# A graph-attention kernel: a planner that keeps VectorE's two-operand steps and GpSimd's sums apart, five places for streamed factors in the last group, and beta x W2 off TensorE

## The chip, the cores and the metric

The kernel runs on one core of a Trainium2 chip, all in float32. The metric is device time in microseconds (us), the median of three runs.

## What is computed

128 graphs of 64 nodes with 512 features each pass through four layers. Each layer adds to x what it makes of h = relu(layernorm(x)). Cut to what matters:

```python
# layer 0: two hypergraph convolutions with a layer norm between, H = (adj != 0)
h1 = relu(Dn * H @ (Be * H.T @ (h @ W1.T)) + b1)
h1 = layer_norm(h1) * gamma + beta
x += Dn * H @ (Be * H.T @ (h1 @ W2.T)) + b2 + h
# layer 1: s = h @ w @ a; A = exp(lrelu(8*tanh((s_i + s_j)/8))) * adj, its rows made to sum to those of adj
x += A @ h @ w
# layer 2: attention
P = adj * exp(q @ k.T)              # q = h @ Wq.T + bq, k = h @ Wk.T + bk
x += (P / P.sum(-1)) @ (h @ Wv.T + bv)
# layer 3: t = normalized adj * exp(lrelu(si + sj + ab)), from h @ Wv3
x += relu(sum over k = 0, 1, 2 of (t^k @ h) @ Wk3[k] + bk3[k])
```

Dn and Be are the reciprocal degrees of nodes and hyperedges. The term beta @ W2.T is a constant row. The kernel makes it once, at the start.

## The kernel before

**Tiling.** A group is 8 graphs: four tiles x of 128 rows (two graphs) by 512. There are 16 groups. All groups pass through layers 0 and 1 first (stage one) and are stored to DRAM (xm, L885). Then all pass through layers 2 and 3 (stage two), where x is read back (x_mid, L346 and L986). The large products are written as Strassen products. L682 is the matmul of layers 0 and 1, whose operand sums are VectorE's (L674). L921 is that of layer 2, with its sums at L907, and L1112 that of layer 3. L583 multiplies a tile by a block-diagonal 128x128 matrix of edge weights, which VectorE writes (L864 in layer 1).

**Layer 3's factors.** The seven combinations of Wk3 are made in stage one and stored to DRAM (fac). In stage two each group streams all of them in again, in 14 loads at L1104: seven of 768 KB (four blocks) and seven of 576 KB (three). They go into places named wf, of which there are three. A place is free again when the matmuls at L1112 that read it are done. Each load needs the place and, by the planner's rule, nothing else. Ahead of these products a group makes its transition matrix t (scores L750 to L756, exponential L1012, L1013 to L1019, 32x32 transposes L1027), its square (L1037, copied at L1039), and t h and t^2 h (L1058). Scores go from a column to a row by way of DRAM (across: a store at L720, two loads at L724); for the last group TensorE does that (L742).

**Who sums.** VectorE makes Strassen sums in SBUF with two SBUF operands (L674, L907, L1082, L1095 to L1097), also L382 (dot products), L700, L864, L960 and L1147. Its other steps read one operand from PSUM (L652, L654, L702, L712, L877, L1131, L996). GpSimd, which is POOL in the profile, has wide sums in SBUF (L710, L798, L799, L876, L973, L1126, L1140 to L1143) and three small steps on single columns for each layer norm (L555, L556, L561).

**The order.** No loop order of the program decides when something runs. Every step is put into a graph (Graph.op) with its engine, a cost in us, what it reads and writes, and a priority. Graph.run plays the steps through in a model of the engines: at every turn it takes the step that can start first, of equals the one of least priority number, and gives it a buffer. The model's start times then set the order in which all instructions are issued, each engine working in order. A step's result counts as there after its cost and a latency (for DMAs, cost is the time on SP's queue). The priority numbers come from a table AT with one entry for each part of the program, from STRETCH (how fast the number grows within a layer) and from PERIOD1 and PERIOD2 (how far groups are apart). The model knows one resource per engine; it lets a VectorE step and a GpSimd step run at the same time whatever they read.

Where the model leaves TensorE idle for over 1 us with a free PSUM bank, fill issues dummy matmuls on a matrix of ones (L1187), FILL = 0.75 of the gap.

**The start.** setup_l0 makes beta x W2 with 8 matmuls of one output row each (L438, two instructions each), copies the row (L440), scales W2 by gamma in place on ScalarE (L442), and spreads the row over 128 partitions with a matmul of ones (L443, copied at L444). bq_c, the first load of all, is a 2 KB load. setup_l3 and setup_bq make small vectors from weights that are loaded in tmp tiles.

Of the kernel before, what the change touches and what calls it, by code (L numbers as in the profile page):

```python
# [11 lines left out]
ALU = mybir.AluOpType  # L12
AX = mybir.AxisListType

P = 128
# [20 lines left out]
class Op:  # L36
    __slots__ = ("eng", "cost", "fn", "prio", "bufs", "npre", "succ", "ready", "seq", "lat")


class Graph:  # L40
# [11 lines left out]
    def op(self, eng, cost, fn, r=(), w=(), lat=None):  # L52
        o = Op()
        o.lat = self.LATENCY[eng] if lat is None else lat
# [28 lines left out]
    def run(self, slots, after, fill):  # L83
# [17 lines left out]
        at = dict.fromkeys(self.ENGINES, 0.0)  # L101
# [4 lines left out]
        while left:  # L106
            best = None
            for e in self.ENGINES:

                can = []  # L110
                for o in open_[e]:
                    t = max(o.ready, at[e])
# [26 lines left out]
            at[o.eng] = t + o.cost  # L139
            end = t + o.cost + o.lat  # L140
# [28 lines left out]
def tile_adj_preln_d4(  # L169
# [95 lines left out]

    def act(cost, fn, r, w):
        return G.op("ACT", cost, fn, r, w)

# [6 lines left out]
    def quad(b):  # L275
        return b.t.rearrange("p (c k) -> p c k", c=4)

    FILL, LAT = 0.75, 2.5


    STRETCH, PERIOD1, PERIOD2 = (1.9884, 2.1221, 50.9861, 3.7462), 79.959, 161.557
    AT = {
        "x0": -2165.99, "apart": 359.07, "w1": 560.57, "b1": -128.79, "w2": 2266.0, "w": 629.08, "c1": 83.74, "l0":
        -235.81, "c2": 158.31, "l1": 2264.36, "c": -2424.06, "g0": -2117.86, "g1": -2122.8, "g2": -1819.53, "g3":
        -591.79, "g": -1886.72, "bq": -99.87, "l3": -7.89, "wg": -1139.97, "wp": 573.47, "beg0": -142.55, "beg1":
        62.01, "end00": -13.21, "end01": -32.01, "end11": -18.15, "new2": -7.11, "new3": -54.85, "end2": -9.77,
        "end3": 676.8, "load1": 485.14, "load2": 547.59, "m": -43.8, "h0": -30.46, "p0": -0.2, "z0": -80.08, "q0":
        9.15, "y0": -548.45, "h1": -32.41, "p1": -27.07, "z1": -26.16, "q1": -1.17, "y1": 3.58, "s": -28.4, "t0":
        14.62, "e0": 9.6, "t1": 5.71, "e1": -125.7, "hT": 311.43, "sh": 220.57, "lq": 604.06, "pt": 684.45, "v":
        70.12, "pv": 723.21, "s3": 659.55, "tt": 692.85, "a0": 741.32, "b0": -508.03, "a1": 777.21, "ws": 323.28,  # L290
        "load3": 129.62, "bk": 350.9,
    }

    def part(name):
        G.shift = AT[name]
# [42 lines left out]
    def load_group(g, src, apart=0.0):  # L338
        b = Buf("adj")
        dma(256, lambda: nc.sync.dma_start(b.t, adj[g]), [], [b])  # L340
        adjs[g] = b
        for t in range(T):
            xx = Buf("x")
            at, key = src(g, t)
            G.shift += apart
            dma(256, lambda xx=xx, at=at: nc.sync.dma_start(xx.t, at), key, [xx], lat=LAT if src is x_mid else 2.0)  # L346
            xt[g, t] = xx
# [7 lines left out]

    part("x0")
    bq_c = load_cols("bq_c", bq, KD)
# [22 lines left out]
    def dot(in0, in1, acc, r, w):  # L380
        j = Buf("o")
        dve(0.77, lambda: nc.vector.scalar_tensor_tensor(j.t, in0(), 1.0, in1(), op0=ALU.mult, op1=ALU.mult,  # L382
                                                         accum_out=acc()), r, [*w, j])

    def combine(name, w_, x_, kc, n, eng, olds=()):
# [5 lines left out]
        cost = c_v(kc * n) * (1 if eng == "DVE" else 2)  # L391
        low, high = wkeys(name, 0, kc), wkeys(name, kc, 2 * kc)
        T1 = (name, "T1")
        G.op(eng, cost, lambda: sub(x_[:, 1], blk(1, 1), blk(0, 1)), [*low, *high], [(name, "x1"), *olds])
        G.op(eng, cost, lambda: sub(blk(0, 1), blk(0, 1), blk(0, 0)), [*low, (name, "x1")], [T1, (name, "given")])
        G.op(eng, cost, lambda: sub(x_[:, 0], blk(1, 1), blk(0, 1)), [*high, T1], [(name, "x0")])
        G.op(eng, cost, lambda: sub(x_[:, 2], blk(1, 0), x_[:, 0]), [*high, (name, "x0")], [(name, "x2")])
# [6 lines left out]
    def combine_hT(name, w_, x_, left):  # L404
# [9 lines left out]
        v = lambda fn, r, w: dve(c_v(D), fn, r, w)  # L414
# [17 lines left out]
    def setup_l0():  # L432

        p, row, pb = Buf("ps"), Buf("o"), Buf("ps")

        def mm():
            for c in range(KH):
# [873 lines left out]
```

## Time and profile before

| what | value |
|---|---|
| median of three runs | 2346.6 us (2346.2 to 2349.21) |
| the profiled execution: its time, its span | 2347.34 us, 2345.6 us |
| TensorE clock granted, mean | 0.998 of full |
| busy: TensorE, VectorE, ScalarE, GpSimd | 2301.3, 1936.0, 1386.6, 1201.9 us |
| filler matmuls (L1187) | 226, 29.3 us busy |
| DMA: moved in all, busy share in 1300-2200 us | 355 MB, 0.81 |
| factor loads, issue to landing | 768 KB 5.8 us, 576 KB 5.0 us (medians) |

Busy time is the union of an engine's instructions. Matmuls are pipelined and their ends are modelled, so the prediction takes the spacing of their starts. Stage one fills the span to about 1200 us and stage two the rest, with groups overlapping at the seam. A group line reads: line, engine, operation, output and inputs by tile name, shapes, count, busy time, mean ns of one, idle time just before and what ended it. A tile name with underscores is memory that several tiles share in turn: w2m_wm_a_wf holds the weights of stage one first, and then a3 and the factor places.

### The profile page before, as it was taken

To read this page: it belongs to the slowest core of one execution; us is meant where nothing else is said; L and a number is where in the kernel's file an instruction comes from. 1 tells how busy PE (TensorE), PEld (TensorE's weight loads), DVE (VectorE), ACT (ScalarE), POOL (GpSimd) and SP (SyncE) were. 2 spreads that over 40 slices of the span, in tenths; PEclk is the share of its full clock that TensorE was granted. 3 is DMA by queue.
4 is the path that set the end of the run, shared out by engine and by line. 5 is a ranking of instruction groups with operands and counts; after the bars stand their busy time and mean duration, and the time that the engine had idled before them with its cause. 6 is when DMAs were issued, how large, how long until landed. Compare 5 with 4: busy or idle time off the path is not lost.

```text
span 2345.6 us, 39929 instructions
## 1 busy us (share of the span) xinstructions
PE 2301.3 (98%) x14342; PEld 1876.8 (80%) x14342; DVE 1936.0 (83%) x4004; ACT 1386.6 (59%) x1986; POOL 1201.9 (51%) x1764
## 2 busy tenths in 40 slices
PE   9999999999999999999999999999999999999998
PEld 4676667776777767777688989999999999999998
DVE  7977887878878777787867888888889888888886
ACT  4656565665656756557556656655565656556642
POOL 5435566556565455553433554455455545455533
PEclk9999999999999999999999999999999999999999
DMA  7333342432333432223334888787888888798767
GB/s 265 85 76 74 82 103 72 106 83 72 95 84 99 89 77 69 70 73 66 89 89 134 235 230 224 211 223 207 242 231 220 230 213 215 211 252 227 214 184 234
DMA packets 403478, 355.13 MB, mean 151 GB/s; under 512 B 290896, under 2 KB 321872, under 8 KB 403280
## 3 DMA queue, kind: packets, MB, share of 16 engines
q1 hardware_dynamic: 403280, 352.58, 56.2%
q8 instruction: 113, 1.85, 0.3%
q14 instruction: 85, 0.70, 0.1%
HBM read 241.05 MB, written 44.33 MB: 122 GB/s over the span
## 4 chain that ended last, share of the span: by engine, by line
PE 75%; DMA 9%; DVE 9%; ACT 3%; POOL 2%; issue 2%; SPq 0%; DVEq 0%; POOLq 0%; ACTq 0%
PE ps L682 35%; PE ps L921 13%; PE ps L1112 13%; PE ps L583 5%; DMA w2m_wm_a_wf<-fac 4%; PE ps L1058 2%; PE ps L990 2%; DVE o L382 2%; PE ps L835 2%; DMA x<-xm 2%; PE ps L952 1%; DVE st L553 1%; DMA wa_q<-o 1%; PE ps L468 1%; DMA rw<-row 1%
## 5 line engine op out<-in xcount | busy, mean ns | idle before, releaser
L574 ACT ACTIVATE h<-x,nm,rs 128x512 f32<-128x512 f32 x384 | 307.0, 814 | 260.7 <-POOL nm L561 234.8
L1112 PE MATMUL ps<-w2m_wm_a_wf 128*128 128x128 f32 x2304 | 300.0, 276 | 3.8 <-DMA w2m_wm_a_wf<-fac 3.1
L1112 PEld LDWEIGHTS ps<-w2m_wm_a_wf 128*128 128x128 f32 x2304 | 279.4, 192 | 9.0 <-issue 2.0
L555 POOL TENSOR_SCALAR rs<-mv 128x1 f32<-128x1 f32 x320 | 102.5, 320 | 349.0 <-DVE mv L554 329.6
L682 PE MATMUL ps<-w2m_wm_a_wf,s_s_zz 128*128 128x256 f32 x1152 | 279.8, 380 | 0.7 <-DVE s_s_zz L674 0.5
L1112 PE MATMUL ps<-w2m_wm_a_wf,tmp_mB_xi 128*128 128x128 f32 x2016 | 262.3, 275 | 3.3 <-ACT h L574 1.7
L682 PEld LDWEIGHTS ps<-w2m_wm_a_wf,s_s_zz 128*128 128x128 f32 x1152 | 216.4, 190 | 48.1 <-issue 18.7
L1112 PEld LDWEIGHTS ps<-w2m_wm_a_wf,tmp_mB_xi 128*128 128x128 f32 x2016 | 244.9, 192 | 6.1 <-ACT h L574 3.0
L682 PE MATMUL ps<-w2m_wm_a_wf,rT_vu_tt 128*128 128x256 f32 x1024 | 237.2, 379 | 3.7 <-ACT rT_vu_tt L594 3.6
L682 PE MATMUL ps<-wa_mem,mT_sx 128*128 128x512 f32 x512 | 236.6, 593 | 0.2 <-ACT mT_sx L585 0.2
L682 PEld LDWEIGHTS ps<-w2m_wm_a_wf,rT_vu_tt 128*128 128x128 f32 x1024 | 193.2, 190 | 44.6 <-issue 12.4
L556 POOL TENSOR_TENSOR rs<-rs,mhalf 128x1 f32<-128x1 f32 x320 | 213.5, 667 | 26.6
L553 DVE BATCH_NORM_STATS2 st<-x 128x6 f32<-128x512 f32 x256 | 173.2, 680 | 17.0 <-DMA x<-xm 11.2
L682 PE MATMUL ps<-wa_mem,s_s_zz 128*128 128x512 f32 x384 | 180.0, 597 | 0.5 <-DVE z_hT L702 0.4
L682 PEld LDWEIGHTS ps<-wa_mem,mT_sx 128*128 128x128 f32 x512 | 96.9, 190 | 102.0 <-issue 96.6
L561 POOL TENSOR_SCALAR nm<-mv,rs 128x1 f32<-128x1 f32 x320 | 160.9, 504 | 30.4
L710 POOL TENSOR_TENSOR u<-u,row_sh 128x256 f32<-128x256 f32 x96 | 77.7, 822 | 170.7 <-DVE u L652 142.3
L592 ACT COPY o<-h 128x1024 uint16<-128x1024 uint16 x128 | 133.4, 1043 | 48.0 <-DVE h L1049 25.2
L583 PEld LDWEIGHTS ps<-bd,h 128*128 128x128 f32 x1024 | 128.7, 194 | 35.0 <-issue 17.1
L973 POOL TENSOR_TENSOR u<-u,wp_bv_bk 128x512 f32<-128x512 f32 x48 | 63.9, 1332 | 181.0 <-ACT u L625 180.8
L594 ACT COPY rT_vu_tt<-z_hT 128x1024 uint16<-128x1024 uint16 x128 | 147.8, 1160 | 10.8 <-DMA z_hT<-tmp_mB_xi 9.7
L822 ACT ACTIVATE z_hT<-z_hT,nm,rs 128x512 f32<-128x512 f32 x128 | 103.8, 813 | 73.3 <-POOL nm L561 73.3
(195 smaller groups left out, 5085.5 us busy)
## 6 DMA issues: line engine op xcount, KB each, us to landing
w2m_wm_a_wf<-fac SPq DMA_DIRECT2D x112, 768.0 KB, 5.8
w2m_wm_a_wf<-fac SPq DMA_DIRECT2D x112, 576.0 KB, 5.0
x<-xm SPq DMA_DIRECT2D x128, 256.0 KB, 3.9
x<-in_x_dram SPq DMA_DIRECT2D x64, 256.0 KB, 2.8
xm<-x SPq DMA_DIRECT2D x64, 256.0 KB, 2.3
out_dram<-x SPq DMA_DIRECT2D x64, 256.0 KB, 4.1
adj<-in_adj_dram SPq DMA_DIRECT2D x32, 256.0 KB, 4.2
fac<-wp_bv_bk SPq DMA_DIRECT2D x63, 128.0 KB, 2.0
```

The lines of the kernel that those rows point to most:

```text
L553: dve(0.69, lambda i=i: nc.vector.bn_stats(st.t[:, i, :], src(i)), [r[i]], [(st, i)])
L555: pool(0.32, lambda: nc.gpsimd.tensor_scalar_add(rs.t, mv.t[:, 1:2], EPS), [mv], [rs])
L556: pool(0.65, lambda: nc.gpsimd.tensor_tensor(rs.t, rs.t, mhalf, ALU.pow), [rs], [rs])
L561: pool(0.47, lambda: nc.gpsimd.tensor_scalar(nm.t, mv.t[:, 0:1], rs.t, -1.0, op0=ALU.mult, op1=ALU.mult), [mv, rs], [nm])
L574: act(0.82, lambda: nc.scalar.activation(h.t, xx.t, AF.Relu, bias=nm.t, scale=rs.t), [xx, nm, rs], [h])
L583: nc.tensor.matmul(quad(p)[:, c, :], h.t[:, c * P:(c + 1) * P], rhs(), start=True, stop=True)
L592: act(1.05, lambda: nc.scalar.copy(u16(planes.t).rearrange("p (q c) -> p q c", q=2), u16(src()).rearrange("p (c q) -> p q c", q=2)), ksrc, ...
L594: act(1.16, lambda: nc.scalar.copy(u16(dst()).rearrange("p c (k q) -> p c k q", q=2), u16(back()).rearrange("p (q c r) -> p c r q", q=2, c ...
L682: nc.tensor.matmul(p.t[:, :n], lhs()[:, c, :], rhs(c), start=first and c == 0, stop=c == kc - 1, skip_group_check=True)
L822: act(0.72, lambda half=half, rs=rs, nm=nm: nc.scalar.activation(half(), half(), AF.Identity, bias=nm.t, scale=rs.t), [(z, j), rs, nm], [( ...
L921: nc.tensor.matmul(pair(p.t)[:, o, :], a, b, start=first and o == 0 and c == 0, stop=c == 1, skip_group_check=True)
L1112: nc.tensor.matmul(inner(p, q)[:, r, :], at()[:, k, :], w_.t[:, r, k, :], start=first and r == 0 and k == 0, stop=k == 2, skip_group_check ...
```

## The change

1. Every step has a port number. GpSimd's steps and VectorE's steps with two SBUF operands (new helper dvp) and some tensor_scalar steps have 1, GpSimd's small steps (new helper small) have 2. In the model, a step with a port number starts no earlier than 0.14 us ahead of the end of the last step with number 1, and only steps with number 1 set that time.
2. Costs in the model are replaced by others: for example 1.43 and 1.39 us for the sums of L798 and L799 by 1.32, factor loads 2.21 and 1.66 us of queue by 2.63 and 2.24, the DMA latency of stage two 2.5 by 2.3, and the trip over DRAM in stage two 3.8 and 4.0 us of latency by 2.3 each.
3. AT, STRETCH, PERIOD1, PERIOD2 are new throughout, so the order on all engines is new; FILL is 0.5.
4. In the last group the 14 factor loads go in turn to five places: the three wf places, the memory of sh and that of hT (both of layer 2). Each of these loads also waits for the last group's squared transition matrix (L1039).
5. Beta x W2: ScalarE multiplies the 8 blocks of W2 by beta (one activation each, in tiles h and o), GpSimd adds them up in 7 sums, and the closing matmul sums over 128 rows of ones rather than one.
6. The load of bq_c takes a later priority than the first x tiles.

```diff
-    def op(self, eng, cost, fn, r=(), w=(), lat=None):
+    def op(self, eng, cost, fn, r=(), w=(), lat=None, port=0):
         o = Op()
+        o.port = port or (1 if eng == "POOL" else 0)
...
-                    t = max(o.ready, at[e])
+                    t = max(o.ready, at[e], port - 0.14) if o.port else max(o.ready, at[e])
...
             at[o.eng] = t + o.cost
+            if o.port == 1:
+                port = t + o.cost
...
+    def dvp(cost, fn, r, w):
+        return G.op("DVE", cost, fn, r, w, port=1)
...
+    def small(cost, fn, r, w):
+        return G.op("POOL", cost, fn, r, w, port=2)
...
-    FILL, LAT = 0.75, 2.5
+    FILL, LAT = 0.5, 2.3
...
-    STRETCH, PERIOD1, PERIOD2 = (1.9884, 2.1221, 50.9861, 3.7462), 79.959, 161.557
+    STRETCH, PERIOD1, PERIOD2 = (2.4612, 8.078, 75.6572, 3.3564), 83.325, 154.352
...
-        def mm():
-            for c in range(KH):
-                nc.tensor.matmul(p.t[0:1, :], gb2[:, 1, c:c + 1], w2_sb[:, c, :], start=(c == 0), stop=(c == KH - 1))
-        pe(c_mm(512, KH), mm, ["gb2b", *wkeys(w2m, 0, KH)], [p])
-        act(0.6, lambda: nc.scalar.copy(row.t[0:1, :], p.t[0:1, :]), [p], [row])
+        for c in range(KH):
+            b = Buf("h") if c else row
+            act(0.65, lambda c=c, b=b: nc.scalar.activation(b.t, w2_sb[:, c, :], AF.Copy, scale=gb2[:, 1, c:c + 1]), ["gb2b", (w2m, c // 2)], [b])
+            if c:
+                pool(1.35, lambda b=b: nc.gpsimd.tensor_add(row.t, row.t, b.t), [b, row], [row])
...
-        pe(c_mm(512, 1), lambda: nc.tensor.matmul(pb.t, ones[0:1, :], row.t[0:1, :], start=True, stop=True), [row], [pb])
+        pe(c_mm(512, 1), lambda: nc.tensor.matmul(pb.t, ones, row.t, start=True, stop=True), [row], [pb])
...
-        dma(4, lambda: nc.sync.dma_start(d, col()), r, [key], lat=lat + 1.3 if lat > 2 else 2.0)
+        dma(4, lambda: nc.sync.dma_start(d, col()), r, [key], lat=lat)
...
-        dma(128, back, [key], [b], 1.2, lat + 1.5 if lat > 2 else 2.0)
+        dma(128, back, [key], [b], 1.2 if lat == 2.0 else 0.7, lat)
...
-                w_, p, q = Buf("wf"), banks[chain][n], len(BLOCKS[n])
+                w_, p, q = Buf(("wf", "sh", "wf", "hT", "wf")[(2 * f + n) % 5] if g == NG - 1 else "wf"), banks[chain][n], len(BLOCKS[n])
...
-                dma(q * 210, lambda n=n, w_=w_, q=q: nc.sync.dma_start(
-                    w_.t[:, :q].rearrange("p r k c -> p (r k c)"), fac[f - 1][n]), [("fac", f - 1, n, k, d) for k in range(3) for d in FACS[n]], [w_], lat=LAT)
+                dma(1000 if q == 4 else 850, lambda n=n, wv=wv: nc.sync.dma_start(
+                    wv(), fac[f - 1][n].rearrange("p (r k c) -> p r k c", k=3, c=P)), [("fac", f - 1, n, k, d) for k in range(3) for d in FACS[n]] + ([(tt, 1)] if g == NG - 1 else []), [w_], lat=LAT)
```

## The prediction, made before the changed kernel was run

> **What bounds the kernel now.** I read the busy shares, then the chain of work that ended last, then the matmuls in order of time.
>
> ```profile
> PE 2301.3 (98%) x14342; PEld 1876.8 (80%) x14342; DVE 1936.0 (83%) x4004; ACT 1386.6 (59%) x1986; POOL 1201.9 (51%) x1764
> PE   9999999999999999999999999999999999999998
> ...
> 1468.25 4.69 PE ps L1112 x42
> 1472.93 10.36 PE ps L921 x48
> ```
>
> TensorE never rests for long, so the time is its work plus what it waits. I split the two by start-to-start spacing, since the ends are modelled. The chain's two lines give 4.69/42 = 0.1117 us for 128 columns and 10.36/48 = 0.2158 for 256. In the same way 512 columns take 0.429, and L1058's matmuls 0.059. The counts of the groups by shape are 5728, 4736, 1080 and 1024: 639.8 + 1022.0 + 463.3 + 60.3. The 64-column forms (L952, L781, L1037) add some 53. **Useful: 2239 us.** The span is 2345.6. The other 107 are 226 filler matmuls (25 us; they too stand where work was missing), 1.0 ahead of the first matmul, 6.1 after the last (2339.5), and stalls of some 75. With the spacings subtracted matmul by matmul, the stalls are 79, and by stage (us):
>
> 0-300: stalls 19.1, fillers 8.3. 300-1100: 9.2, none. 1100-1300: 9.7, 12.3. 1300-2200: 32.5, none. 2200-2346: 8.7, 4.7.
>
> So layers 0 and 1 in their steady stretch are within 1.2% of TensorE's own work. A better order can earn only in the start, the change of stage, layers 2 and 3, and the end. Of the stalls over 0.3 us, about 21 end on a DVE result (L864 7.7, L907 4.7, L1131 4.3, the rest small) and 12.4 on factor loads.
>
> ```profile
> PE ps L1112 <- DMA w2m_wm_a_wf<-fac: 7.0, 11, 1.3
> ...
> 2302.98 5.57 PE ps L1112 x48
> 2308.56 4.30 DMA w2m_wm_a_wf<-fac
> 2313.00 4.94 PE ps L1112 x42
> 2317.95 5.50 DMA w2m_wm_a_wf<-fac
> 2323.58 4.94 PE ps L1112 x42
> 2328.54 5.90 DMA w2m_wm_a_wf<-fac
> ```
>
> The first line is TensorE's waits in 1300-2200; the rest is the chain's end, where loads and matmuls take turns.
>
> **What the skill says.** "SBUF — State Buffer", section "Who interferes with whom": a VectorE instruction with two SBUF inputs and a GpSimd instruction that reads SBUF exclude each other, and whoever starts second waits for the whole other instruction. This trace agrees:
>
> ```profile
> 33.19 0.77 DVE L700 SCALAR_TENSOR_TENSOR u<-u,col,row_sh 128x512 f32<-128x512 f32 x1
> 33.37 3.38 POOL L798 TENSOR_TENSOR x<-x,h 128x512 f32<-128x512 f32 x2
> 34.65 2.66 DVE L700 SCALAR_TENSOR_TENSOR u<-u,col,row_sh 128x512 f32<-128x512 f32 x2
> ...
> L960 DVE TENSOR_TENSOR bd<-ee,adj 64x256 f32<-64x256 f32 x32 | 27.9, 870 | 0.9
> L1019 DVE TENSOR_TENSOR bd<-ee,col 64x256 f32<-64x256 f32 x32 | 13.9, 434 | 1.0
> ```
>
> Two L700 beside the sums of L798 take 2.66 us, not 1.5; L960 costs twice L1019 at one shape. Compared with the median of the same form with no sum beside it, DVE loses 134 us in all and POOL 100. Forms that read PSUM lose nothing (L877: 0.42 either way).
>
> "TensorE: Matmul & The Clock Gate", section "What's actually happening": a window of some 3.4 us without work halves the clock. The trace has a case: after a filler block and 2.08 us of idleness the 32 matmuls of L583 at 151.44 took 5.40 us, while those at 1167.13 took 3.84.
>
> **The change, part by part.**
>
> *Beta x W2.* Goes: 16 matmuls.
>
> ```profile
> 43.60 7.03 PE L438 MATMUL ps<-w2m_wm_a_wf,gb 128*1 128x512 f32 x16
> ```
>
> That is 6.96 us start to start, and ACT's 0.56 copy. Comes: 8 activations of 128x512 on ACT (0.61 us apart at L442: 4.9 us) and 7 POOL sums of that shape (L799: 1.27 alone, 1.40 mean: 9-10 us). The closing matmul keeps its columns. On the path: freed at 43.6, TensorE's next product needs a DVE sum (L674) that ends at 47.15, and the first W2 product at 61.4 needs a DVE result of 61.57. So about half of the 6.96 turns into waiting. ACT is idle 4.2 us ahead of 48.5 and W2 has landed by then (issued 38.8, median 5.6), which covers most of its added work; without that cover the scaling of W2 comes up to 4.9 us later. POOL's sums are due when L712 first reads the row, at 72.5; they queue among L799's sums and the row statistics of later tiles. **Taken -3, between -7 and +3.**
>
> *Five places.* In the last group TensorE uses a half product in 4.69/2 = 2.35 us on average, and a place is refilled in 5.4 (mean of the medians 5.8 and 5.0). Three places turn in 7.05 us where 2.35 + 5.4 = 7.75 are needed; five turn in 11.75. The five waits at the end (0.45, 0.36, 0.38, 0.91, 0.20, each with some 0.14 of restart) are 3.0 us, and the ring was their cause. The rate allows it narrowly: 9.63 MB in 32.9 us are 293 GB/s, and 2306-2334 moved 257 with 79% of the engines' time. The price is a new wait: each of these loads now waits for the second transition matrix (L1039, done at 2299.1). Before, three were issued from 2290.2 and had landed by 2301.0, ahead of the first product at 2302.9. From 2299.1 a load lands at 2303.4 (the fastest near the end, 4.3) to 2304.9. Behind the waiting load on SP stand transposes and output stores. -3 and +1: **taken -2**, between -6 (the matrix is made earlier, and the fillers at 2295 go too) and +4.
>
> *Fillers.* Factor 0.75 to 0.5: about 150 in place of 226, 8 us. In nearly all blocks the next matmul's last input came under 0.3 us before its start, so fillers displaced no work. **Taken 0**, between -1 and +3.4 (two cold restarts like 151.44).
>
> *bq_c's load* leaves the head of the queue: 0.46 us of issue at most, taken 0.
>
> *The order.* Instructions are otherwise the same. The planner now starts a two-operand DVE step or a POOL step only when the last holder of the port is done, has measured costs, charges the big loads by bandwidth (2.63 and 2.24 us of queue, before 2.2 and 1.66), and all priorities are new. The chip did the excluding before as well; what can be won is that DVE does its PSUM steps while POOL sums, so that results for TensorE are less late. DVE at 83% has little spare, so its 134 blocked microseconds matter more than they would on ACT. I take half of the 21 us that end on DVE and a quarter of the 8.8 of factor waits before the end: -10.5 and -2. Against it, a shorter assumed row trip (below) +1.5. **Taken -11**, between -40 and +30.
>
> **Sum:** -3 -2 +0 -11 = -16 on the profiled execution's 2347.3 (span 2345.6 and 1.7 around). The median of the runs is 0.7 lower: 2346.6 - 16 = **2330.6**.
>
> **The rivals.** *A far better order.* The 21 us on DVE vanish, half of the 22 in 1100-1300, 6 at the end, and beta's 7 come whole: -45, near 2302. For it: 107 us are not work. Against: a third of the stalls are under 0.3 us each, which no order removed.
>
> *No change.* The port excluded already, beta's time becomes waiting, the new load wait eats the gain of the places: 2344-2350.
>
> *Slower, through the row trip.* In layer 3 the sums of scores go to DRAM and come back as rows. The old planner reckoned 0.34 + 3.8 + 1.2 + 4.0 = 9.3 us; the new one 0.34 + 2.3 + 0.7 + 2.3 = 5.6. From 1260 to 2240 the trace shows
>
> ```profile
> rw<-row SPq DMA_DIRECT2D x30, 64.0 KB, 5.3
> row<-col SPq DMA_DIRECT2D x14, 2.0 KB, 3.7
> ```
>
> and 10.4 us for the whole trip. The plan is then 4.8 us short in 15 groups, 72 us. L752 waits for the row at the head of DVE; S-sums, L1131 and statistics stand behind it, and TensorE behind them. If half reaches TensorE, +36 against -16: near 2366. It decides once over 16 of 72 us (22%) get through. Against: the bandwidth charge on loads ahead of the row gives some of it back, and other groups' work lies between.
>
> **Chances.** Forecast (2318-2341) 0.50; far better 0.20; no change 0.10; slower 0.20. 0.2% is 4.7 us, about what a measurement of this kernel can tell from no change, so faster means under 2341.9. Faster 0.70, same 0.10, slower 0.20. The range 2298 to 2364 leaves out the better half of the second case and the worse half of the fourth.
>
> **What would show it.** Right: no L438, next matmuls in its place within 4 us; no wait for factors in the last 30 us; DVE's 134 blocked us down by a third or more with PSUM steps beside POOL's sums; stalls plus fillers near 95. Wrong: L752 waiting over 2 us per group with TensorE idle on DVE behind it; DVE's busy time unchanged; a wait of several us ahead of the last group's first product.

## The result, and the profile after

The changed kernel takes 2342.8 us (median of 19 runs, 2337.8 to 2347.0). Its ratio to the kernel before is **0.9983, with a 95% interval of 0.9975 to 0.9990**: about 4 us faster, where 16 were forecast. The profiled execution took 2345.87 us with a span of 2344.1. Several sets of runs follow, and in them the kernel before had medians of 2347.3 to 2350.8. So all comparisons below are ratios to the kernel before in the same set; where one is told in us, it is the ratio's difference from 1 (or from 0.9983, for "than the kernel after") times 2346.6. The kernel after ran in the first set alone, so a comparison with it goes by way of the kernel before and is uncertain by some 3 us.

Lines move by 9 to 12: L682 is now L691, L921 L930, L1112 L1124, L583 L592, L674 L683, L864 L873, L907 L916, L752 L761, L960 L969, L1019 L1028, L1095 L1104, L1131 L1143, L468 L477, L1187 L1199. In the experiments that start from the kernel before, lines move by up to 4 (L685 in b_beta_none and L1115 in b_five are L682 and L1112).

From the page after, the busy times and TensorE's slices:

```profile
PE 2292.1 (98%) x14280; PEld 1873.0 (80%) x14280; DVE 1859.1 (79%) x4004; ACT 1388.6 (59%) x1993; POOL 1201.2 (51%) x1771
PE   8999999999999999999999999999999999999997
```

VectorE is busy for 77 us less with the same instructions. Most of that is waiting on the shared port which the order now avoids: the prediction's count of blocked time gives 55 of it. The group that showed it best before, L960 at 27.9 us and 870 ns, is now equal to its twin. The groups by line:

```profile
L1028 DVE TENSOR_TENSOR bd<-ee,col 64x256 f32<-64x256 f32 x32 | 14.4, 449 | 1.0
L969 DVE TENSOR_TENSOR bd<-ee,adj 64x256 f32<-64x256 f32 x32 | 13.3, 416 | 0.5
```

By that count VectorE's blocked time fell from 134 to 79 us (41%) and GpSimd's from 100 to 81. The rows of scores come back faster as well, where the third rival had put its price. DMA issues of 1260 to 2240 us (count, KB, median us to landing):

```profile
rw<-row SPq DMA_DIRECT2D x30, 64.0 KB, 3.3
row<-col SPq DMA_DIRECT2D x14, 2.0 KB, 3.3
```

So two fifths of the blocking went. But TensorE, which sets the time, hardly gained. Its waits on VectorE in 1300-2200 before (us in all, times, longest), and then its waits there after:

```profile
PE ps L1112 <- DVE s_s_zz L1131: 2.8, 4, 0.8
PE ps L921 <- DVE row_sh L907: 2.8, 7, 0.5
```

```profile
PE ps L1124 <- DMA w2m_wm_a_wf<-fac: 8.9, 11, 2.3
PE ps L1124 <- DVE s_s_zz L1143: 0.8, 1, 0.8
```

The VectorE waits of the middle stretch have nearly gone, and the factor waits of this trace are longer (7.0 before); in 2200-2346 they are 4.0 us, where they were 2.6. The chain's last line is one block without a wait, where loads and matmuls took turns before:

```profile
2323.09 14.35 PE ps L1124 x126
```

The start has become worse. TensorE's timeline before, then after:

```profile
7.93 8.80 PE L468 MATMUL ps<-tmp_mB_xi 128*128 128x512 f32 x16 [2.95 <-DMA tmp_mB_xi<-in_Wk_dram]
```

```profile
8.64 5.37 PE L477 MATMUL ps<-tmp_mB_xi 128*128 128x512 f32 x8 [3.82 <-DMA tmp_mB_xi<-in_Wk_dram]
...
22.62 5.21 PE L477 MATMUL ps<-tmp_mB_xi 128*128 128x512 f32 x8 [1.59 <-DMA tmp_mB_xi<-in_Wk_dram]
```

And SP's queue, before and then after:

```profile
2.11 0.43 SPq L329 DMA_DIRECT2D tmp_mB_xi<-in_Wk_dram  x1
```

```profile
0.72 1.82 SPq L355 DMA_DIRECT2D x<-in_x_dram  x4
...
3.53 0.44 SPq L338 DMA_DIRECT2D tmp_mB_xi<-in_Wk_dram  x1
```

Four x tiles go ahead of the first weights. The two halves of W1, both issued at 7.82 us before, are issued at 21.50 and 29.08 after, and the first product that needs them (L682, now L691) starts at 32.10 instead of 28.54. TensorE has done 12.9 us of useful work by 30 us instead of 18.7.

With the spacings of the prediction, taken matmul by matmul (the prediction's 2239 us were taken by counts), TensorE's time divides as follows (us). "Ended by" tells what a stall of over 0.3 us ended on; gaps are the stalls of under 0.3 us each.

| | useful | fillers | stalls | ended by VectorE | factor loads | other loads | ScalarE | gaps |
|---|---|---|---|---|---|---|---|---|
| before | 2233.3 | 25.2 | 79.2 | 21.9 | 12.4 | 3.1 | 8.7 | 33.0 |
| after | 2226.4 | 20.1 | 88.7 | 19.8 | 16.1 | 6.6 | 10.3 | 35.4 |

6.9 us of work went (beta x W2) and 5.1 of fillers, and 9.5 of stalls came. These are two single executions, and the one after is 3 us above its kernel's median. Part of the 9.5 is the clock. In the execution before, TensorE's granted clock was 0.50 for 3.4 us at a time twice (from 8.0 and 151.3 us), in the one after five times (from 8.7, 22.3, 80.3, 1302.3 and 1667.5). By the spacings the matmuls in these stretches lost 2.8 us before and 7.5 after, spread over the columns of the table. The last one follows a wait for a factor. From the timeline after, twelve matmuls at full clock and twelve of the same form after that wait; then engines' busy time, clock and DMA in the stretch:

```profile
1660.19 1.50 PE L1124 MATMUL ps<-w2m_wm_a_wf,tmp_mB_xi 128*128 128x128 f32 x12
...
1667.13 2.54 PE L1124 MATMUL ps<-w2m_wm_a_wf,tmp_mB_xi 128*128 128x128 f32 x12 [2.08 <-DMA w2m_wm_a_wf<-fac]
```

```profile
1667.50:1670.90 3.40, 3.40 (x18) 3.40 (x18) 1.95 (x5) 0.81 (x1) 0.72 (x1) 0.50 1.16 190
```

How often this happens differs between executions of one order: a_nosum, below, lost 2.8 us in this way and a_three 8.6. The mean granted clock over the 19 runs is 0.9967; the kernel before had 0.9974 to 0.9977 in the later sets. So in a usual run the clock's share is smaller than in this pair, some 2 us by estimate (0.0008 of the time).

How far is the kernel after ahead, in useful work done and with the 6.9 left out of the sum before? By 300 us 3.7 us, so that some 3 of the 6.9 are lost at the start; by 1100, 3.3; by 1300, 3.5; by 2200, 6.6; at the end 1.5 (the spans). So stage one's steady stretch and the seam of the stages (1100-1300) give nothing, layers 2 and 3 give 3, and the end takes back 5.

### The profile page after: what moved, and what is told of

The parts are those of the page before. It is cut to its first block, busy times and chain, and to the rows that moved or that the text cites. A ratio compares the mean times of both kernels' runs of the same rounds, so it can differ in the third digit from the quotient of the medians.

```text
span 2344.1 us, 39830 instructions
## 1 busy us (share of the span) xinstructions
PE 2292.1 (98%) x14280; PEld 1873.0 (80%) x14280; DVE 1859.1 (79%) x4004; ACT 1388.6 (59%) x1993; POOL 1201.2 (51%) x1771
## 4 chain that ended last, share of the span: by engine, by line
PE 79%; DMA 6%; DVE 4%; ACT 3%; issue 1%; POOL 1%; SPq 0%; DVEq 0%; ACTq 0%; POOLq 0%
PE ps L691 34%; PE ps L1124 18%; PE ps L930 15%; PE ps L592 4%; DMA w2m_wm_a_wf<-fac 3%; PE ps L844 2%; PE ps L1067 2%; PE ps L999 2%; PE ps L961 1%; DMA adj<-in_adj_dram 1%; DMA rw<-row 1%; ACT h L583 1%; DMA h<-o 1%; ACT o L601 1%; DVE st L562 1%
## 5 line engine op out<-in xcount | busy, mean ns | idle before, releaser
L583 ACT ACTIVATE h<-x,nm,rs 128x512 f32<-128x512 f32 x384 | 308.6, 816 | 251.3 <-POOL nm L570 233.9
L564 POOL TENSOR_SCALAR rs<-mv 128x1 f32<-128x1 f32 x320 | 118.3, 371 | 388.0 <-DVE mv L563 362.1
L1124 PE MATMUL ps<-w2m_wm_a_wf 128*128 128x128 f32 x2256 | 295.7, 276 | 5.1 <-DMA w2m_wm_a_wf<-fac 4.5
L1124 PEld LDWEIGHTS ps<-w2m_wm_a_wf 128*128 128x128 f32 x2256 | 277.1, 193 | 10.3 <-issue 2.9
L691 PE MATMUL ps<-w2m_wm_a_wf,s_s_zz 128*128 128x256 f32 x1152 | 276.9, 379 | 4.5 <-DVE s_s_zz L683 4.0
L1124 PE MATMUL ps<-w2m_wm_a_wf,tmp_mB_xi 128*128 128x128 f32 x1968 | 259.0, 277 | 10.1 <-DMA w2m_wm_a_wf<-fac 6.6
L691 PEld LDWEIGHTS ps<-w2m_wm_a_wf,s_s_zz 128*128 128x128 f32 x1152 | 217.1, 190 | 52.4 <-issue 18.9
L1124 PEld LDWEIGHTS ps<-w2m_wm_a_wf,tmp_mB_xi 128*128 128x128 f32 x1968 | 239.4, 193 | 15.3 <-issue 4.9
L691 PE MATMUL ps<-w2m_wm_a_wf,rT_vu_tt 128*128 128x256 f32 x1024 | 240.0, 381 | 4.1 <-ACT u L659 2.4
L691 PE MATMUL ps<-wa_mem,mT_sx 128*128 128x512 f32 x512 | 239.1, 593 | 0.8 <-DMA wa_mem<-in_W1T_dram 0.5
L691 PEld LDWEIGHTS ps<-w2m_wm_a_wf,rT_vu_tt 128*128 128x128 f32 x1024 | 193.7, 191 | 42.9 <-issue 11.3
L565 POOL TENSOR_TENSOR rs<-rs,mhalf 128x1 f32<-128x1 f32 x320 | 208.6, 652 | 25.3
L691 PE MATMUL ps<-wa_mem,s_s_zz 128*128 128x512 f32 x384 | 181.1, 595 | 1.4 <-DVE z_hT L711 1.4
L691 PEld LDWEIGHTS ps<-wa_mem,mT_sx 128*128 128x128 f32 x512 | 96.0, 190 | 106.5 <-issue 98.8
L603 ACT COPY rT_vu_tt<-z_hT 128x1024 uint16<-128x1024 uint16 x128 | 146.6, 1159 | 18.1 <-DMA z_hT<-tmp_mB_xi 17.9
L592 PEld LDWEIGHTS ps<-bd,h 128*128 128x128 f32 x1024 | 127.4, 192 | 25.7 <-DVE bd L873 10.5
L601 ACT COPY tmp_mB_xi<-z_hT 128x1024 uint16<-128x1024 uint16 x128 | 133.7, 1045 | 9.3 <-issue 3.0
```

The costliest lines, as they stand in the source:

```text
L564: small(0.28, lambda: nc.gpsimd.tensor_scalar_add(rs.t, mv.t[:, 1:2], EPS), [mv], [rs])
L565: small(0.62, lambda: nc.gpsimd.tensor_tensor(rs.t, rs.t, mhalf, ALU.pow), [rs], [rs])
L583: act(0.82, lambda: nc.scalar.activation(h.t, xx.t, AF.Relu, bias=nm.t, scale=rs.t), [xx, nm, rs], [h])
L592: nc.tensor.matmul(quad(p)[:, c, :], h.t[:, c * P:(c + 1) * P], rhs(), start=True, stop=True)
L601: act(1.05, lambda: nc.scalar.copy(u16(planes.t).rearrange("p (q c) -> p q c", q=2), u16(src()).rearrange("p (c q) -> p q c", q=2)), ksrc, ...
L603: act(1.16, lambda: nc.scalar.copy(u16(dst()).rearrange("p c (k q) -> p c k q", q=2), u16(back()).rearrange("p (q c r) -> p c r q", q=2, c ...
```

## The experiments

**What the port costs.** *b_nosum* is the kernel before with each wide GpSimd sum cut to its first column and two memsets put in its place, which read nothing from SBUF; *a_nosum* is the same in the kernel after.

```diff
-                pool(1.43, lambda xx=xx, h=h: nc.gpsimd.tensor_add(xx.t, xx.t, h.t), [h, xx], [xx])
+                pool(1.43, lambda xx=xx, h=h: wide(xx.t, xx.t, h.t), [h, xx], [xx])
...
+    def wide(o, a, b, sub=False):
...
+        for _ in range(2):
+            nc.gpsimd.memset(o, 0.5)
```

> The kernel before, order untouched, but each of GpSimd's wide sums is replaced by a sum of its first column and two fills of the same tile with a constant, which take about as long and read nothing (so the sums of all layers are left out). VectorE is then hardly ever blocked: its 134 us of blocked time should fall below 20. If blocked time is what makes VectorE's results late for TensorE (the reason for half of 21 us in the prediction), this is at least 10 us faster, toward 2330. If the late results are late for other reasons (trips over DRAM, chains at the seams of the stages), it stays within 5 us of 2346.6 though VectorE gets over 100 us freer.

> The changed kernel, order untouched, with GpSimd's wide sums replaced as in the other run (a sum of the first column and two fills that read nothing; the sums are left out). The plan already keeps the two apart, but 79 us of blocked VectorE time are left on the chip. If the rest of the blocking costs TensorE, 5 or more us faster than 2342.8; if blocking is off the path, within 3 us of it.

Measured: b_nosum 0.9952 (0.9938 to 0.9965), **11.3 us** faster; a_nosum 0.9965 (0.9953 to 0.9977), 4.2 us faster than the kernel after. The busy times of b_nosum:

```profile
PE 2302.5 (99%) x14342; PEld 1879.6 (81%) x14342; DVE 1780.4 (76%) x4004; ACT 1383.9 (59%) x1986; POOL 1194.3 (51%) x3132
```

GpSimd is as busy as before and VectorE has 156 us less, so the stand-in takes away the blocking and leaves the queue as it was. TensorE's stalls that end on VectorE go from 21.9 to 10.2 us in b_nosum, and from 19.8 to 15.2 in a_nosum. The port's part of them was thus 11.7 us before and is 4.6 after: the change recovered about 7. The times say the same (11.3 and 4.2 us), though the 4.2 carries an uncertainty of some 3 us. The part that has nothing to do with the port rose from 10.2 to 15.2 in these traces. By VectorE's busy time the blocking itself was 156 us before and is 86 after (1859.1 in the kernel after, 1772.7 in a_nosum).

**Beta x W2.** *b_beta_one* is the kernel before with one of the eight matmuls.

```diff
-            for c in range(KH):
-                nc.tensor.matmul(p.t[0:1, :], gb2[:, 1, c:c + 1], w2_sb[:, c, :], start=(c == 0), stop=(c == KH - 1))
+            nc.tensor.matmul(p.t[0:1, :], gb2[:, 1, 0:1], w2_sb[:, 0, :], start=True, stop=True)
```

> The kernel before, its plan and order untouched, with one of the eight matmuls of beta x W2 issued (leaves out seven eighths of that product). This takes 14 instructions, 6.1 us, from TensorE at 43.6. If they stood on TensorE's path, 2346.6 falls by about 6 to 2340.5. If the start is bound by other results, as the prediction reckoned, by about half, 2343.5. If the whole stretch waits for something else anyway: 2346.6, and TensorE's stalls near 47 and 61 grow by 6.

Measured: 1.0006 (0.9994 to 1.0018), no gain from 6.1 us less work. The trace says why; in TensorE's waits of the first 60 us the largest is

```profile
PE ps L442 <- ACT o L439: 6.1, 1, 6.1
```

L442 is the spreading matmul of the same step (L443 before). It waits for ScalarE's copy of the row, which has its turn no sooner than before. So this run had moved the time within the step. The wait also had a price behind it: the granted clock is 0.66 in 50-60 and 0.82 in 60-70 us, where the kernel before has 1.00. *b_beta_none* takes that wait away too:

```diff
-        pe(c_mm(512, 1), lambda: nc.tensor.matmul(pb.t, ones[0:1, :], row.t[0:1, :], start=True, stop=True), [row], [pb])
+        def flat():
+            for c in range(4):
+                nc.tensor.matmul(pb.t[:, c * P:(c + 1) * P], ones[0:1, :], ident[0:1, :], start=True, stop=True)
+
+        pe(c_mm(512, 1), flat, [row], [pb])
```

> The kernel before with one of the eight matmuls of beta x W2, as in b_beta_one, and the matmul that spreads the row over the partitions put on data that is there from the start (four of 128 columns in place of one of 512, the same columns in all), so that it waits for nothing; its result is not the row of beta x W2. In b_beta_one TensorE stood 6.1 us at that spreading matmul, for ScalarE's copy of the row, which was still queued: what was taken out came back as a wait inside the same step. Theory A (the step as a whole costs the old order its 7 us, and b_beta_one only hid that): 5 to 8 us faster than the kernel before, 2339 to 2342 us. Theory B (without that wait the matmuls behind it would stand as long for the next thing, so that the old order hides the step): within 2.5 us of the kernel before.

Measured: 1.0023 (1.0015 to 1.0032), 5.4 us **slower**, which neither theory had. TensorE's timeline in b_beta_none:

```profile
60.37 3.78 PE L685 MATMUL ps<-w2m_wm_a_wf,rT_vu_tt 128*128 128x256 f32 x8 [3.41 <-ACT rT_vu_tt L597]
...
69.61 3.65 PE L685 MATMUL ps<-w2m_wm_a_wf,rT_vu_tt 128*128 128x256 f32 x8 [2.73 <-ACT rT_vu_tt L597]
...
81.85 1.89 PE L685 MATMUL ps<-w2m_wm_a_wf,s_s_zz 128*128 128x256 f32 x8
```

The next products wait for ScalarE's operand, as theory B had it. Then the eight matmuls take 3.78 us where the same form takes 1.89 later on: the granted clock is 0.67 in 60-70 and 0.84 in 70-80 us, where the kernel before has 1.00. This agrees with the Trainium skill, "TensorE: Matmul & The Clock Gate", section "What's actually happening", by which an idle window of some 3.4 us halves the clock, as far as the halving goes. But the clock was halved here after 2.73 us of idleness as well, and after 2.08 in the kernel after (shown above) and in the prediction's case at 151.44; all three are shorter than the page's window, and the measurement decides. By the count of useful work, with the 6 us that were taken out left aside, b_beta_none is 4.3 us behind the kernel before by 300 us; where the rest arises is not shown. *a_beta8* goes the other way, in the new order:

```diff
+        def summed():
+            for c in range(KH):
+                nc.tensor.matmul(pb.t[0:1, :], ones[:, 0:1], row.t, start=True, stop=True)
+            nc.tensor.matmul(pb.t, ones, row.t, start=True, stop=True)
...
-        pe(c_mm(512, 1), lambda: nc.tensor.matmul(pb.t, ones, row.t, start=True, stop=True), [row], [pb])
+        pe(c_mm(512, 1), summed, [row], [pb])
```

> The kernel after with its order untouched; ahead of the one matmul that puts the rows of beta x W2 over the partitions, TensorE gets eight more of one output row (128 x 1 by 128 x 512), whose results the next matmul writes over, so that TensorE pays again what the change took from it (14 to 16 instructions, about 7 us). Theory A (in the new order too the start waits for the weights of the first stage to land and for the chain of the first tiles behind them, so that 7 us of TensorE's work at 54 us go into its idle time): 2342 to 2344 us, within 1.5 us of the kernel after. Theory B (the new order has its idle time elsewhere, and the step that my prediction put at -3 us is in the result): 2347 to 2350 us, 5 to 7 us more than the kernel after. TensorE's useful work up by about 7 us either way; under A the stalls and fillers of the first 300 us fall by as much.

Measured: 1.0016 (1.0008 to 1.0025), **7.7 us slower than the kernel after**, give or take 3: theory B, and all of the step's work counts. The order of the kernel after, with TensorE's part of the step given back, is thus 3.8 us slower than the kernel before (1.9 to 5.9). The eight matmuls stand behind the row that ScalarE and GpSimd make, not where the old ones stood, and that other work stays; so this is the step's price at that place.

**The five places.** *b_five* puts the places and the new wait into the kernel before; *a_three* takes the places, not the wait, out of the kernel after.

```diff
-                w_, p, q = Buf("wf"), banks[chain][n], len(BLOCKS[n])
+                w_, p, q = Buf(("wf", "sh", "wf", "hT", "wf")[(2 * f + n) % 5] if g == NG - 1 else "wf"), banks[chain][n], len(BLOCKS[n])
```

> The kernel before with the five places and their wait in the last group alone. The plan is the same up to the first load of the last group. By the prediction: 2 us faster (3 of load waits gone, 1 lost to the later first load). Rival: the loads are bound by the rate of the DMA engines and can't start ahead of the transition matrix, so five places only let them queue, and the first product waits: 2 to 10 us slower.

> The changed kernel with three places in the last group instead of five, its loads still waiting for the transition matrix. The order up to the last group is the same. If five places earn what the prediction says (3 us of load waits), this is 3 us slower than 2342.8. If the loads are bound by the rate from the matrix on, it is within 1 us.

Measured: b_five 1.0053 (1.0039 to 1.0067), 12.4 us slower; a_three 0.9977 (0.9968 to 0.9987), no slower than the kernel after. SP's queue at the end of b_five, and then TensorE's timeline:

```profile
2299.55 6.88 SPq L1107 DMA_DIRECT2D w2m_wm_a_wf<-fac  x3
...
2313.85 3.76 SPq L593 DMA_TRANSPOSE wa_q<-o  x1
```

```profile
2314.64 7.98 PE L1190 MATMUL ps<-ones 128*128 128x128 f32 x70
2326.36 1.36 PE L1115 MATMUL ps<-w2m_wm_a_wf,tmp_mB_xi 128*128 128x128 f32 x6 [3.74 <-DVE tmp_mB_xi L1095]
```

The last transpose of the group, issued at 2303.55 in the kernel before, now stands behind loads that wait for places, until 2313.85. ScalarE reads what it brings at 2322.70, VectorE's sums follow, and TensorE has 8 us of fillers and 3.7 of waiting. In 2298-2314 SP waits 8.7 us for products that free a place and less for other things, but never for the matrix. The new wait stands in the planner alone, and on the chip it acts only by the order of SP's queue. In b_five that order puts the first load at 2297.40 instead of 2290.18, and the first product waits 1.94 us for it. In the kernel after the first load goes out ahead of the matrix (L1048, at 2296.2), and the others stand behind two output stores, for whose data SP waits 6.2 us, and behind the last transpose (at 2299.66):

```profile
2292.39 0.52 SPq L1116 DMA_DIRECT2D w2m_wm_a_wf<-fac  x1
2298.76 0.81 SPq L1163 DMA_DIRECT2D out_dram<-x  x2
...
2301.01 0.57 SPq L1116 DMA_DIRECT2D z_hT<-fac  x1
```

With three places in this order the end looks much the same. From 2298 us on TensorE waits for factors for 2.2 us in a_three and 1.5 in the kernel after; in the kernel before it was 2.3 from 2302 on. The chain of a_three has the same last block without a wait:

```profile
2321.55 14.39 PE ps L1124 x126
```

**Fillers.** *b_fill_half* is the kernel before with the new factor.

```diff
-    FILL, LAT = 0.75, 2.5
+    FILL, LAT = 0.5, 2.5
```

> The kernel before with FILL at 0.5, order untouched: a third fewer fillers. As predicted, no change (within 1 us). If fillers displaced ready work, up to 3 us faster; if the clock falls in the longer gaps, up to 3 us slower and a lower granted clock at 146 to 156.

Measured: 0.9998 (0.9987 to 1.0009). Fillers cost nothing: 150 are left, 8.4 us less of them, and by the same spacings about 10 us more of stalls have come in their place. This bears on the table above. With the old order and the same loads, the factor waits of this trace are 15.8 us where they were 12.4.

**What waits for factors cost.** *b_short* and *a_short* load only the first block of each factor load from the second group on.

```diff
-                    wv(), fac[f - 1][n].rearrange("p (r k c) -> p r k c", k=3, c=P)), [("fac", f - 1, n, k, d) for k in range(3) for d in FACS[n]] + ([(tt, 1)] if g == NG - 1 else []), [w_], lat=LAT)
+                    wv()[:, :1] if g else wv(), fac[f - 1][n].rearrange("p (r k c) -> p r k c", k=3, c=P)[:, :1 if g else None]), [("fac", f - 1, n, k, d) for k in range(3) for d in FACS[n]] + ([(tt, 1)] if g == NG - 1 else []), [w_], lat=LAT)
```

> The kernel before with the factor loads cut in the same way (products of later groups use old factors). Its stalls on factors are 12.4 us and its row trips take 10.4 us. If the loads are what stretched the trips and made the order run late against its plan in the second stage, the gain is above 12 us, up to 25; if only the direct waits count, about 12.

> The changed kernel, order untouched, in which every factor load after the first group's fetches only its first block of 192 KB instead of four or three (so the products of all later groups use old factors). If the factor loads hold up TensorE only where the profile says so, this is 13 to 16 us faster (14.8 us of stalls on them). If they also delay the trips over DRAM, the transposes and x, more, 20 us or over. If queue waits are hidden, under 5.

Measured: b_short 0.9947 (0.9935 to 0.9958), 12.4 us faster than the kernel before; a_short 0.9915 (0.9902 to 0.9927), 16.0 us faster than the kernel after. In b_short no factor wait of over 0.3 us is left, in a_short 3.3 us are; the stalls of all kinds fall by 13.5 and 18.1 us. So these waits, 12.4 and 16.1 us in the table, are worth about themselves. That the change made them longer is not shown: the two gains differ by no more than their uncertainty, and the old order has 15.8 us with fewer fillers (b_fill_half).

**Is it the rule or the table?** *a_oldtable* is the kernel after with the shifts, stretches and periods of the kernel before.

```diff
-    STRETCH, PERIOD1, PERIOD2 = (2.4612, 8.078, 75.6572, 3.3564), 83.325, 154.352
+    STRETCH, PERIOD1, PERIOD2 = (1.9884, 2.1221, 50.9861, 3.7462), 79.959, 161.557
```

> The kernel after with the planner's new rule and costs, but with the old table of 69 shifts and the old stretches and periods. It computes the same. Theory A (rule and table belong together: the old table leaves the two-operand work and the sums of the two engines in one another's way, and the planner, which now excludes them, makes each wait for the other): near the planner's own reckoning, 2538 us, with TensorE stalls of 200 us or more, spread over the stages. Theory B (the rule alone makes the order better, and the table only trims it): 2335 to 2350 us.

Measured (two runs): 1.0866 (1.0840 to 1.0892), 203 us slower: rule and table belong together. For the other four runs I searched for other tables, with the planner's own reckoning as the aim: small random changes of some entries at a time, kept when the reckoning fell (or, early on, rose only a little). *a_search* and *a_search2* change only the table of the kernel after; the difference is in the lines of AT and in

```diff
-    STRETCH, PERIOD1, PERIOD2 = (2.4612, 8.078, 75.6572, 3.3564), 83.325, 154.352
+    STRETCH, PERIOD1, PERIOD2 = (2.520041, 12.017701, 75.643155, 3.224665), 84.86769, 154.14132
```

> The kernel after with nothing changed but the planner's table of shifts, stretches and periods, which were searched on with its own model for 20 minutes: its reckoning goes from 2341.0 to 2325.6 us, with the same rule, costs, places and work. It computes the same. Theory A (the rule was worth what I forecast, the table of the kernel after lost it again in the order of transfers and starts; the model, whose reckoning of the kernel after is 3 us below its span, can be followed down): 2325 to 2333 us. Theory B (the chip's waits for transfers, which land 4 to 8 us after their issue where the model counts 2.3 us and the bytes, take the place of what the model saves): 2337 to 2344 us, no better than the kernel after.

> The kernel after with only the table changed again: the search of a_search carried on for 25 minutes, the planner's reckoning from 2325.6 to 2319.8 us. It computes the same. Theory A (with the rule in it the model can be followed further down; of the 15.4 us it promised in a_search the chip gave 9.5): 0.6 of the further 5.8, so 3.5 us faster than a_search, 2332 to 2336 us. Theory B (what is left of the promise is eaten by waits for transfers): within 1.5 us of a_search, 2336 to 2340 us.

*a_ruleoff* has its own table and the line

```diff
-                    t = max(o.ready, at[e], port - 0.14) if o.port else max(o.ready, at[e])
+                    t = max(o.ready, at[e])
```

> The kernel after with the planner's rule taken out (an operation that needs the shared port no longer waits for the other engine's in the plan) and a table that was searched on for it, as long as the one of a_search, from where that one ended; places, beta x W2, costs and fillers as in the kernel after. The planner's reckoning without the rule is 2295.6 us. It computes the same. Theory A (the rule is what made an order better, because a plan that can't see the port promises what the chip doesn't give): the promise fails by 45 us or more, 2341 to 2352 us, VectorE's blocked time back to 120 us or more. Theory B (it was the search, and any search earns the same; the rule gives nothing of its own): 2333 to 2340 us, like a_search, with VectorE's blocked time above that of the kernel after.

*b_search* is the kernel before with only its table searched.

> The kernel before with only its table changed, searched on with its own model (no rule, old costs) for 20 minutes as a_search was: its reckoning goes from 2312.3 to 2299.2 us. It computes the same. Theory A (a model that doesn't see the port can't be followed down): 2343 to 2352 us, within 3.5 us of the kernel before on the one side and slower on the other. Theory B (search alone earns): 2334 to 2340 us, 8 us or more faster than the kernel before.

Measured (the span is that of the profiled execution; VectorE is its busy time, which is 1780 in b_nosum, where the wide sums are gone; stalls are TensorE's; all but the ratio in us):

| | rule | planner's reckoning | span | ratio to before | VectorE | stalls, fillers |
|---|---|---|---|---|---|---|
| before | no | 2312.3 | 2345.6 | 1 | 1936 | 79, 25 |
| b_search | no | 2299.2 | 2343.9 | 0.9983 (0.9974 to 0.9992) | 1941 | 88, 15 |
| a_ruleoff | no | 2295.6 | 2354.9 | 1.0031 (1.0016 to 1.0047) | 1922 | 111, 9 |
| after | yes | 2341.0 | 2344.1 | 0.9983 (0.9975 to 0.9990) | 1859 | 89, 20 |
| a_search | yes | 2325.6 | 2336.6 | 0.9943 (0.9928 to 0.9957) | 1853 | 86, 16 |
| a_search2 | yes | 2319.8 | 2321.5 | **0.9901** (0.9884 to 0.9919) | 1854 | 71, 15 |

Without the rule the reckoning ends 33 to 59 us ahead of the chip, and the lower the search brings it the larger the gap. With the rule it ends 2 to 11 us ahead (0 to 10 by the medians of all runs), and following it down pays. a_search2 beats both kernels: 23 us faster than before, 19 than after. It gained 9.9 us over a_search where the reckoning fell by 5.8; neither expectation had so much, and some of it may be luck. By the ratios a_search comes to 2333 us and b_search to 2343, both at the edge of their theory A, and a_ruleoff to 2354, slower than its theory A had it. Each row is one table, and before and b_search have the old costs as well. a_ruleoff and a_search differ in the rule and in what one search found with it. b_search has the ratio of the kernel after with none of its parts: a search of the old table alone also gives 4 us. What the plan without the rule can't see shows in TensorE's waits, a_ruleoff first and then a_search2:

```profile
PE ps L930 <- DVE row_sh L916: 12.9, 14, 2.0
PE ps L691 <- DVE s_s_zz L683: 9.2, 8, 2.9
```

```profile
PE ps L691 <- DVE s_s_zz L683: 3.0, 5, 1.3
```

The sums L916 that a_ruleoff waits for take 1100 ns in the median there, and 689 in the kernel after; in b_search, where they are L907, they take 1216 (min, median and max of one of the line's two forms, in a_ruleoff, after and b_search):

```profile
L916 DVE TENSOR_TENSOR row_sh<-row_sh,z_hT x32: 676/1100/1216, 1196.3 to 2235.0; 128x512 f32<-128x512 f32 x32
```

```profile
L916 DVE TENSOR_TENSOR row_sh<-row_sh,z_hT x32: 677/689/1103, 1183.1 to 2219.5; 128x512 f32<-128x512 f32 x32
```

```profile
L907 DVE TENSOR_TENSOR row_sh<-row_sh,z_hT x32: 683/1216/1256, 1190.1 to 2220.6; 128x512 f32<-128x512 f32 x32
```

This is the mechanism that the Trainium skill has in "SBUF — State Buffer", section "Who interferes with whom", and these are the traces' prices of it for one instruction. Where did a_search2 win? By the same ledger as above it is ahead of the kernel before by 5.4 us at 300, 5.6 at 1100, 18.6 at 1300 and 27.7 at 2200, and gives back 3.6 at the end. The largest part, 13 us, is the seam, where fillers and stalls are 8.8 us against 22.0 before and 23.0 after. Some 7 to 9 of the 13 are had without the rule: fillers and stalls there are about 13 us in b_search and 15 in a_ruleoff. What b_search wins there it loses again in layers 2 and 3: it is ahead of the kernel before by 6 us at 1100, 15 at 1300 and 4 at 2200, and in 1300-2200 TensorE waits for the sums L907 for 7.7 us where it was 2.8. a_search2 keeps its gain through layers 2 and 3; that this is the rule's part is likely by these waits, but not shown apart from the search. a_ruleoff is behind the kernel before by 12 us at 1100 already; how much of that is the port no run separates.

## Why the prediction was right or wrong

The direction was right, and the size was not: 4 us where 16 were forecast. The step that failed is **"The order … taken −11"**. It took half of all waits on VectorE as won and let the rest stand; the change removed only part of the port's share, and the new order brought waits of its own.

*The order.* The kernel after with the step of beta x W2 given back (a_beta8) is 3.8 us slower than before. In it are the order, the places and the fillers; the last two are worth about nothing here (a_three, b_fill_half), so the order cost some 4 us where the forecast had 11 of gain. By its terms, from the two profiled executions:

- "half of the 21 us that end on DVE", −10.5. Right was that blocking is half of them: b_nosum removes all blocking and 11.7 of the 21.9 with it. But the step priced the whole removal, and the change removed 41% of VectorE's blocked time (45% by busy time). The port's part fell by 7.1 (11.7 to 4.6). And the other half, which I had let stand, grew by 5.0: a new order is late in new places. Net: −2.1.
- "a quarter of the 8.8 of factor waits", −2. They did not fall: 12.4 before and 16.1 after, +3.7 in this pair, of which fewer fillers can be the cause (15.8 in b_fill_half). Nothing in the rule bears on them.
- Not in the sum at all: other loads, those of weights at the start above all, +3.5; ScalarE's results, +1.6; gaps and the rest, +2.8. Of these only the first stands out in the other traces too (6.6 to 9.1 us in those of the new order, 2.7 to 4.4 in those of the old). The clock was not in the sum either: 4.7 of the 9.5 lie in stretches at half clock. Against these stand 5.1 fewer fillers.

−2.1 + 3.7 + 3.5 + 1.6 + 2.8 is the 9.5 of stalls; less 5.1 gives +4.4, beside the 3.8 that a_beta8 shows. That these two come so near is in part luck, since the profiled execution after is a slow one of its kind. I had treated the order as the old one with one fault mended. It was a new one, of which only the sum over all waits can be told. Where this table is late at the start and the end is seen (x and other loads ahead of the weights; the last group's second load behind stores that wait, with 10 fillers and 1.2 us of waiting ahead of 2305.64). That the rule does not stand in the way of a better time is shown by a_search2, which has the rule and another table.

*Beta x W2*, taken −3, between −7 and +3. In the new order it is worth about 7.7, at the better end; in the old one it would have been worth nothing or less. The reasoning (half turns into waiting on what comes next) fits the old order better, where b_beta_none shows the wait for L597 (L594 before) and not half but all of it lost. One reading in it can't stand: the first W2 product starts at 61.39, ahead of the VectorE result of 61.57 that it was said to need; what it waits for when TensorE comes early is that operand of ScalarE. And the step had to be priced in the order in which it would stand, and that was not to be seen. The clock after the wait was not in the step; the prediction had seen such a case and priced it only for fillers.

*Five places*, taken −2, between −6 and +4. Measured in the old order +12.4, in the new one about 0. "The ring was their cause" is not borne out: with three places a_three waits 2.2 us there, with five the kernel after still waits 1.5, and both run their last 126 matmuls without a wait. The wait for the matrix, priced at +1, is not one on the chip; it moves the loads in SP's queue. And the text named "transposes and output stores" behind the waiting load and then priced only the load; in the old order the transpose was the larger cost.

*Fillers*, taken 0: right (180 are left in the new order, not 150). *The load of bq_c*, taken 0: not tried alone.

*The rivals.* "Slower, through the row trip" is out: the trip took 7.1 us in stage two where 10.4 were measured before, and VectorE waits at L761 for 1.9 us in all of 1300-2200. The row's load lands in 3.3 us where it took 5.3; why, no run tells. "No change" came nearest in time; of its reasons, that the places gain nothing held, but not through a wait for the matrix, and beta's time turned into waiting in the old order alone. "A far better order" was not this kernel, but it was open: a_search2 does what that rival said of the seam, and by its 23 us half of what it said in all.

*The signs named.* No L438: yes. VectorE's blocked time down by a third, and its busy time with it: yes. Stalls plus fillers near 95: no, 109. No factor wait in the last 30 us: nearly, the last ends at 2317.6. A wait ahead of the last group's products: not before the first, but before the fourth (2305.6).

What stays open: what the rule is worth by itself, since a_search and a_ruleoff, 20 us apart, are one searched table each; why the part of VectorE's waits that is not the port's grew; and how the +4 of the order divides, which single traces tell only roughly.

## What to carry to other kernels

Price a shared resource by an experiment or a count of what would be late without it, and take only the share that the change removes. A planner's rule is worth what its plan can then be trusted for: compare the plan's end with the chip's, before and after, and search again once they agree. And price a wait by everything queued behind it on the issuing engine, the transposes first.

## What the runs showed of the hardware that was not expected

- Removing 6 us of work from the busiest engine made the kernel 5 us slower. Two idle stretches of 3.4 and 2.7 us came in its place, and the clock was 0.67 in 60-70 and 0.84 in 70-80 us (b_beta_none).
- A wait of 2.08 us was enough to be followed by 3.4 us at half clock: the next 12 matmuls took 2.54 us instead of 1.50 (after, at 1667.13).
- Blocking that costs VectorE 134 us of its own time by the count, or 156 by its busy time in b_nosum, costs the kernel 11.3 us.
- Of a load's 768 KB it is the landing time that counts, 5.2 us in the median: TensorE waits for such loads again and again, 12 to 16 us in all, and loading a quarter or a third of each takes nearly all of that away (b_short, a_short).
